# An attention and non-local kernel: v's projection with nested products, softmax denominators taken earlier, another range test

## The chip, the cores and the metric

The kernel runs on one core of a Trainium2 chip. That core has a matrix engine (TensorE, PE in the profile; its weight loads are PEld), a vector engine (VectorE, DVE), a scalar engine (ScalarE, ACT), a general one (GpSimd, POOL), and SyncE (SP), which mostly issues DMA transfers. Sixteen DMA engines do these transfers. The metric is the device time of one launch in microseconds: the median of the runs.

## The reference

Eight images of 512 channels and 32x32 = 1024 pixels pass through two layers, all in fp32. Layer 0 is self-attention with 8 heads of 64 channels and a residual. Layer 1 is a non-local block with a residual, followed by batch norm over all images.

```python
q, k, v = conv1x1(x, Wq, bq), conv1x1(x, Wk, bk), conv1x1(x, Wv, bv)   # 512 -> 512, 8 heads of 64
attn = softmax(einsum('bhdn,bhdm->bhnm', q, k) * 64**-0.5)
x = x + conv1x1(einsum('bhnm,bhdm->bhdn', attn, v), Wp, bp)

g, theta, phi = conv1x1(x, g_w), conv1x1(x, theta_w), conv1x1(x, phi_w)  # 512 -> 256, with biases
f = einsum('bcn,bdn->bcd', theta, phi) / 1024
z = conv1x1(einsum('bcd,bdn->bcn', f, g), W_w, W_b) + x
out = (z - mean(z)) * rsqrt(var(z) + 1e-5) * gamma + beta                # mean, var over images, pixels
```

## The kernel before

**The images in turn.** A loop runs over the images. For image b it does attention (`attention`), then the projections q, v and k of image b+1 in this order (`heads_of`, `values`, `heads_of`), then image b's projection by Wp with the residual (`project`), theta and phi (`theta_phi`), and the rest of the non-local block (`nonlocal_`). The q, k and v of image 0 come before the loop. Batch norm follows at the end (`last_z`).

**Matmuls in fewer products.** A product of two matrices cut 2x2 is done with 7 products of quarters in place of 8 (Strassen's scheme, Winograd's form). `seven` does this; its matmuls stand in line 300. It needs sums of quarters of the weights and of the data. Those of the weights are made once, in image 0 (`weight_sums`), and stored in DRAM beside the quarters as "kept" weights. Each later use loads the whole set again by `load_w` (line 134), in the order of a list `queue`, into one of two buffers. Sums of the data are made on VectorE at each use (`data_sums`, `more_sums`; `inner_parts` for those of a quarter's quarters).

For the weights named in `INNER`, some of the seven products are themselves done by seven smaller ones: three products of WqT and WkT, two of WpT. `nested` does that (line 255). The four large products that stay (`FOUR`) are cut into 16 units, and between these the small steps are interleaved as a table `STEPS` says: none up to unit 2, at most two per unit after that. A dictionary `fills` gives, per unit, VectorE work of other kinds that is to stand there in program order.

PSUM is held as four double banks of 128 x 2 x 512, with tags s0 to s3; a list `free` says which stage takes which one, in what order. A bank is written again only when its last reader is done. q and k are made channel by pixel; v is made pixel by channel ("positions out": the data are the stationary operand, the weights move). In v before, all seven products are of 2 x 4 matmuls with 256 moving columns, 56 in all.

**Attention.** Scores (line 462) and the weighted sums of v (line 488) are matmuls on 64x64 tiles of the array. ScalarE takes the exponential without subtracting a maximum (line 465), and VectorE adds up what the denominators need, eight key blocks into `acc` (lines 469 and 471). For each of eight groups of two heads and half of the pixels, `spread` (lines 499 and 501) folds the 128 partitions of `acc` to 32, by one transfer of SyncE and three accumulating ones of GpSimd, into a buffer `fold`. After every four groups two more transfers fold 128 rows of that to 64.

**Denominators.** `all_denominators` sums the rows of `fold` on TensorE (line 434): two matmuls with 64 columns of a selector `folds8` as weights and 512 moving columns. VectorE takes the reciprocal (line 534, 128x512), SyncE writes one row of each group to DRAM (line 536), and four SyncE transfers of 512 KB read them back into the same buffer, each row spread over 64 partitions (`rows_of`, line 558). Then four multiplications on VectorE (line 571) scale the attention's output `o`. The matmuls, the reciprocal and the transfers are issued after v's product 1 (`norm`), the multiplications after its product 5. The load of k's weights is issued after q, ahead of them, and SyncE issues its transfers one after another in program order. For the last image there is a different path (`denominators`, in two halves), and no further projections.

**The range test.** Since the exponential isn't shifted, the kernel returns whether that was sound; if not, a second kernel (`shifted`) is run. Before, `bound_scores` bounds the scores: the largest |q| and |k| per channel (line 397, eight VectorE reductions an image), a matmul with a matrix `heads` (line 425), a comparison (line 427), and four GpSimd multiplications of q by 0 or 1 (line 429). In the end all flags are reduced.

**Order.** The order of most work is left to a scheduler, which places instructions by program order, readiness and buffers. `pe`, `dve` and `sp` pin an instruction to program order on its engine: all of TensorE's are, and some of VectorE's and SyncE's. The start of image 0 has a fixed VectorE order for the sums that q needs (line 842).

Of the kernel before, what the change touches and what calls it, by code (L numbers as in the profile page):

```python
# [19 lines left out]
BOUND = 60.0  # L20
# [10 lines left out]
def unshifted(ctx: ExitStack, tc: tile.TileContext, a: dict, out: bass.AP):  # L31
# [83 lines left out]
    INNER = {"WqT": (1, 2, 6), "WkT": (1, 2, 6), "WpT": (1, 2)}  # L115
# [8 lines left out]
    def load_w(dma):  # L124

        if not queue:
            return
        name = queue.pop(0)
        half = quarter(name, 0, 0).shape[2]
        t, w = weights_tile(name, half)  # L130
        loaded.append((name, w))
        if name in kept:
            of = kept["plain"] if name == "WpT" and len(queue) == 2 else kept[name]
            ins = dma.dma_start(t[:, :of.shape[1]], of)
            if len(queue) == 1:
                sp(ins)
            return
        corner[name] = block(f"a21_{name}")[:, :, :half]
        for to, m, k in ((w[:, 0], 0, 0), (w[:, 1], 0, 1), (w[:, 2], 1, 1), (corner[name], 1, 0)):
            dma.dma_start(to, quarter(name, m, k))  # L140

    def weights(name, sums_done=False):

        n, w = loaded.pop(0)
        assert n == name
        if name not in kept:
            if not sums_done:
                weight_sums(w, corner[name])
            if name not in ("WqT", "WkT"):
                keep("plain" if name == "WpT" else name, w)  # L150
        return w
# [11 lines left out]
    def keep_inner(name, w):  # L163

        for n in range(len(INNER[name])):
            a11, a12, a22, a21, s2, s3, s4 = inner_blocks(w, name, n)
            for to, l, r, op in ((s3, a11, a21, ALU.subtract), (a21, a21, a22, ALU.add), (s2, a21, a11, ALU.subtract),
                                 (s4, a12, s2, ALU.subtract)):
                nc.vector.tensor_tensor(to, l, r, op)
# [75 lines left out]
    def nested(name, stage, w, data, tags, first, add):  # L245
# [3 lines left out]
        for n, (q, di, begins) in enumerate(goes_to[i] for i in INNER[stage]):  # L249
# [3 lines left out]
            for _, wi, di, s, reads in SEVEN:  # L253
                ps = pair[s % 2 if s < 2 else 1][:, s // 2, n % 2 * 256:(n % 2 + 1) * 256]
                pe(nc.tensor.matmul(ps, a[wi], d[di], start=s not in begun, stop=True, skip_group_check=True))  # L255
                begun.add(s)
                for to, is_first in reads:
                    c = rows(q).start + int(to[0]) - 1
# [4 lines left out]
    def seven(name, w, data, positions_out, first, add, between=None, early=False,  # L263
# [10 lines left out]
        if inner:  # L274
            free[:] = [tags[1], tags[2], tags[3], tags[0]]
            steps = nested(name, inner, w, data, tags[2:], first, add)
# [6 lines left out]
        for n, m in HALVES if three else ((n, None) for n in range(len(products))):  # L283
# [12 lines left out]
            work = [(*part, k) for part in (parts if m is None else parts[m:m + 1]) for k in range(nk)]  # L296
            if by_chunk and what in ("11", "s1t1"):
                work.sort(key=lambda one: one[4])
            for to_ps, at, lhsT, rhs, k in work:
                pe(nc.tensor.matmul(to_ps, lhsT(k), rhs(k), start=(s, at) not in begun, stop=(k == nk - 1),  # L300
                                    skip_group_check=True))
                begun.add((s, at))
                for ahead in (True, False):
# [25 lines left out]
    heads = const.tile([P, P], F32, tag="heads", name="heads")  # L329
    nc.vector.memset(heads, 0.0)  # L330
# [13 lines left out]
    for i in range(WARM):  # L344
        pe(nc.tensor.matmul(ps[:, :P], heads, heads, start=True, stop=True))
# [10 lines left out]
    for i in range(4):  # L356
        nc.vector.memset(folds[i * P // 4:(i + 1) * P // 4, i * D // 4:(i + 1) * D // 4], 1.0)
    folds8 = const.tile([P, D], F32, tag="folds8", name="folds8")
    nc.gpsimd.memset(folds8, 0.0)
    nc.gpsimd.affine_select(out=folds8, in_=folds8, compare_op=ALU.is_gt, fill=1.0, base=1 - P // 8,  # L360
                            pattern=[[-P // 8, 8], [0, D // 8]], channel_multiplier=1)
    nc.gpsimd.affine_select(out=folds8, in_=folds8, compare_op=ALU.is_ge, fill=0.0, base=0,
                            pattern=[[-P // 8, 8], [0, D // 8]], channel_multiplier=1)
    for j in range(2):
        nc.vector.memset(heads[j * D:(j + 1) * D, j * D:(j + 1) * D], 1.0)
    mv = const.tile([P, CC, 2], F32, tag="mv", name="mv")
    gates = const.tile([P, B * NPAIR], F32, tag="gates", name="gates")
# [9 lines left out]
    def heads_of(b, what, w, bias, data, pin=lambda ins: None, later=None, **how):  # L377

        t = mats.tile([P, CC, N], F32, tag=what, name=f"{what}_{b}")
        peak = small.tile([P, CC], F32, tag=f"peak_{what}", name=f"peak_{what}_{b}")  # L380
# [15 lines left out]
        def peak_of(c):  # L396
            ins = nc.vector.tensor_reduce(peak[:, c:c + 1], t[:, c, :], AX.X, ALU.max, apply_absolute_value=True)
            if b == 0 or later is not None:
                dve(ins)

        for c in range(CC):
            if later is None:
                peak_of(c)
            else:
                later.append(lambda c=c: peak_of(c))
        return t, peak

    def values(b, w, data, between=None):
        v = mats.tile([P, NB, C], F32, tag="v", name=f"v_{b}")

        def at(q):
            return v[:, (int(q[1]) - 1) * NB // 2:int(q[1]) * NB // 2, (int(q[0]) - 1) * C // 2:int(q[0]) * C // 2]

        def as_v(ps):
            return ps.rearrange("p h (i f) -> p (h i) f", f=C // 2)

        seven(f"pv_{b}", w, data, True, lambda q, ps: nc.scalar.copy(at(q), as_v(ps)),  # L417
              lambda q, ps: dve(nc.vector.tensor_tensor(at(q), at(q), as_v(ps), ALU.add)), between)
        return v

    def bound_scores(b, q, k, peak_q, peak_k):

        nc.vector.tensor_tensor(peak_q, peak_q, peak_k, ALU.mult)
        ps = next_bank(f"bound_{b}")[:, 0, :]
        pe(nc.tensor.matmul(ps[:, :CC], heads, peak_q, start=True, stop=True))
        gate = gates[:, b * NPAIR:(b + 1) * NPAIR]
        nc.vector.tensor_scalar(gate, ps[:, :CC], BOUND / SCALE, 1.0, ALU.is_le, ALU.mult)  # L427
        for p in range(NPAIR):
            nc.gpsimd.tensor_scalar(q[:, p, :], q[:, p, :], gate[:, p:p + 1], 1.0, ALU.mult, ALU.mult)  # L429
# [6 lines left out]
    def attention(b, q, k, v, near_end, make_f=None):  # L436
# [66 lines left out]
        def spread(u, pin=lambda ins: None, meanwhile=lambda: None):  # L503
# [18 lines left out]
            if i == 3 and not make_f:  # L522
                two = t[:, g, :].rearrange("(r s) n -> s r n", s=2)
                together(t[g * D:(g + 1) * D, 2, :], [two[0], two[1]])

        def all_denominators(ps):
# [4 lines left out]
            t, ps = t[:, 2, :], ps[:, 0, :]  # L531
            columns(ps, folds8, lambda j: t[:, j * 512:(j + 1) * 512])
            ri = t[:, :512]
            nc.vector.reciprocal(ri, ps)
            d = dram2.tile([16, 512], F32, tag="den", name=f"den_d_{b}")
            nc.sync.dma_start(d, ri.rearrange("(a s) n -> a s n", a=16)[:, 0, :])
            d = d.rearrange("(j g i) n -> g j (i n)", j=2, g=2)
            return d[0], d[1]

        def denominators(g, ps):  # L540
# [8 lines left out]
            d = dram2.tile([8, 512], F32, tag=f"den{g}", name=f"den_d_{b}_{g}")  # L549
            nc.sync.dma_start(d, ri.rearrange("(a s) n -> a s n", a=8)[:, 0, :])  # L550
            return d.rearrange("(j i) n -> j (i n)", j=2)
# [8 lines left out]
        def normalize(d):  # L560

            for g in range(2):
                if g not in rows:
                    rows_of(g, d[g])
            r = rows["all"]

            def products():
                for g in range(2):
                    for h in range(NH):
                        at = o["o"][:, 2 * g:2 * g + 2, h * 512:(h + 1) * 512]  # L570
                        dve(nc.vector.tensor_tensor(at, at, r[:, 4 * g + h:4 * g + 4:2, :], ALU.mult))

            return products
# [179 lines left out]
    late, z = {}, {}  # L753
# [90 lines left out]
    q, peak_q = heads_of(0, "q", weights("WqT", True), bq, data, early=True, by_chunk=True)  # L844
    keep_inner("WqT", w_first)
    load_w(nc.sync)
# [5 lines left out]
    w = weights("WkT")  # L852
    k, peak_k = heads_of(0, "k", w, bk, data)
    keep_inner("WkT", w)
    load_w(nc.sync)
    v = values(0, weights("WvT"), data, {3: lambda: bound_scores(0, q, k, peak_q, peak_k)})
    load_w(nc.sync)
    held = {}
    for b in range(B):
# [23 lines left out]
        if not last:  # L883
            later, of_22, of_t4 = [], [], []
# [4 lines left out]
                     8: lambda: (of_22[0](), of_22[1]()), 9: lambda: (of_22[2](), of_22[3]())}  # L889
            q, peak_q = heads_of(b + 1, "q", weights("WqT"), bq, nxt["data"], dve, inner="WqT",  # L890
                                 later=later, fills=fills)
            load_w(nc.sync)

            def norm():
                nxt["products"] = normalize(denominators(next_bank(f"den_{b}")))

            v = values(b + 1, weights("WvT"), nxt["data"], {1: norm, 2: lambda: [one() for one in later], 5: lambda: nxt["products"]()})
# [7 lines left out]
            else:  # L905
                w_p = loaded[1][1]
                for unit, which in ((12, (3, 4)), (14, (5, 6))):
                    fills[unit] = lambda which=which: weight_sums(w_p, corner["WpT"], which, dve)
            later_k = []
            k, peak_k = heads_of(b + 1, "k", weights("WkT"), bk, nxt["data"], later=later_k, inner="WkT",  # L910
                                 fills=fills)
# [3 lines left out]
        else:  # L915
# [4 lines left out]
            normalize(nxt["d"])()  # L920
# [16 lines left out]
        elif b > B - LATE and b != B - 2:  # L937
# [3 lines left out]
                       {5: lambda: b < B - 2 and of_theta.append(f_sums(b, tps[0], 0)), 1: lambda: [one() for one in later_k[:2]], 2: lambda: [one() for one in later_k[2:]],  # L941
                        4: lambda: bound_scores(b + 1, q, k, peak_q, peak_k)})
# [20 lines left out]

    last_z()


    good = const.tile([P, 1], F32, tag="good", name="good")
    nc.vector.tensor_reduce(good, gates, AX.X, ALU.min)
# [215 lines left out]
```

## Time and profile before

| | us |
|---|---|
| median of 3 runs (2145.69 to 2147.35) | 2146.07 |
| span of the profiled execution | 2143.6 |
| busy: TensorE / VectorE / ScalarE / GpSimd | 2119.6 / 1448.4 / 742.8 / 193.2 |
| matmuls of scores (L462), of weighted sums (L488) | 529.4, 528.7 |
| reductions for the peaks, each (L397) | 1.2 |
| GpSimd's multiplications of q, each (L429) | 1.1 |
| from issue to landing: 2368 KB of q's or k's weights | 8.8 |
| from issue to landing: 1792 KB of v's weights | 7.2 |
| from issue to landing: 512 KB of r, each of four | 6.9 |

The profiled execution's span is that of its instructions; the median of the runs lies 2.5 us above it. Busy times are those in which an engine executes; two of them overlap freely. In a group's line, the name left of the arrow is what is written, right of it what is read; then come the shape, the number of instructions, the busy sum and the mean in ns, and the engine's idle time just before them with what ended it. In the chain and in a timeline, a line gives the start in us from the span's beginning and the duration. An image takes about 263 us, so the middle ones can stand for each other.

### The profile page before, as it was taken

The numbers are of one execution on the slowest core, as the hardware profiler recorded it, in microseconds if no ns is written. First come the engines' busy times: TensorE is split into PE (matmuls) and PEld (weight loads), VectorE is DVE, ScalarE is ACT, GpSimd is POOL, SyncE is SP. The second block draws the span as 40 slices with busy tenths as digits, with TensorE's granted clock in tenths as the row PEclk, the third lists the DMA queues.
The fourth block names the chain that finished last, engine by engine and source line by source line (L and its number), as shares of the span: only waits on it lengthen the run. The fifth ranks groups of instructions, "written<-read, shape, count | busy, mean of one in ns | idle before, by whom it ended". The sixth has DMA issues, their size and how long they took to land.

```text
span 2143.6 us, 30444 instructions
## 1 busy us (share of the span) xinstructions
PE 2119.6 (99%) x12654; PEld 1123.3 (52%) x12654; DVE 1448.4 (68%) x1795; ACT 742.8 (35%) x848; POOL 193.2 (9%) x242
## 2 busy tenths in 40 slices
PE   9999999999999999999999999999999999999996
PEld 4534664356733567335673366633666347743462
DVE  6467667667676676766667667676675676756736
ACT  1464104641046310463105621066212652056106
POOL 0111000110001100011001100011000110011000
PEclk9999999999999999999999999999999999999998
DMA  6433443334143331433323342233434235122758
GB/s 242 137 46 58 136 166 127 49 71 129 73 131 49 79 116 73 133 50 83 109 102 109 48 100 99 97 107 50 108 132 161 42 45 139 52 60 39 227 197 341
DMA packets 53969, 231.05 MB, mean 108 GB/s; under 512 B 9792, under 2 KB 16192, under 8 KB 46272
## 3 DMA queue, kind: packets, MB, share of 16 engines
q1 hardware_dynamic: 42144, 199.26, 27.5%
q0 software_dynamic: 10192, 28.46, 11.0%
q8 instruction: 101, 1.65, 0.3%
q10 hardware_dynamic: 1488, 1.32, 0.2%
q14 instruction: 44, 0.36, 0.1%
HBM read 141.84 MB, written 46.27 MB: 88 GB/s over the span
## 4 chain that ended last, share of the span: by engine, by line
PE 96%; ACT 1%; DVE 1%; DMA 1%; issue 0%; SPq 0%; ACTq 0%; DVEq 0%
PE ps L462 21%; PE po L488 21%; PE pv L300 9%; PE ptp L300 9%; PE pp L300 7%; PE pk L300 6%; PE pq L300 5%; PE pg L300 4%; PE pk_in_s L255 3%; PE pq_in_s L255 3%; PE pz L300 2%; PE pf L658 2%; PE pp_in_s L255 2%; PE pwf L713 1%; ACT z L830 1%; PE pf L674 1%
## 5 line engine op out<-in xcount | busy, mean ns | idle before, releaser
L465 ACT ACTIVATE e<-ps 128x1024 f32<-128x1024 f32 x512 | 522.6, 1024 | 431.1 <-PE ps L462 425.6
L471 DVE TENSOR_TENSOR acc<-acc,e 128x1024 f32<-128x1024 f32 x384 | 470.0, 1224 | 143.7 <-ACT e L465 140.3
L462 PE MATMUL ps<-q,k 64*64 64x512 f32 x4096 | 529.4, 589 | 0.0
L488 PE MATMUL po<-e,v 64*64 64x512 f32 x4096 | 528.7, 589 | 0.0
L488 PEld LDWEIGHTS po<-e,v 64*64 64x64 f32 x4096 | 156.6, 133 | 282.9 <-issue 275.4
L462 PEld LDWEIGHTS ps<-q,k 64*64 64x64 f32 x4096 | 155.5, 133 | 283.8 <-issue 274.8
L501 POOL DMA_DIRECT2D fold<-acc x189 | 147.1, 779 | 978.9 <-DMA fold<-acc 576.6
L701 ACT ACTIVATE g<-pg,gb 128x512 f32<-128x512 f32 x31 | 21.3, 687 | 475.4 <-PE pg L300 475.3
L469 DVE TENSOR_TENSOR acc<-e,e 128x1024 f32<-128x1024 f32 x64 | 78.3, 1224 | 136.6 <-ACT e L465 136.6
L300 PE MATMUL pv<-w_WvT,t_x 128*128 128x256 f32 x512 | 116.4, 381 | 0.0
L300 PE MATMUL ptp<-w_tp,t_x 128*128 128x256 f32 x512 | 114.4, 379 | 0.0
L417 ACT COPY v<-pv 128x1024 f32<-128x1024 f32 x32 | 32.4, 1012 | 213.9 <-PE pv L300 213.9
L300 PEld LDWEIGHTS pv<-w_WvT,t_x 128*128 128x128 f32 x512 | 96.6, 190 | 18.5 <-issue 5.7
L300 PEld LDWEIGHTS ptp<-w_tp,t_x 128*128 128x128 f32 x512 | 97.3, 190 | 13.2
L300 PE MATMUL pq<-t_x,w_WqT 128*128 128x512 f32 x200 | 100.1, 592 | 0.8 <-DVE t_x L842 0.8
L300 PE MATMUL pp<-t_o,w_WpT 128*128 128x512 f32 x208 | 100.8, 592 | 0.0
L300 PE MATMUL pk<-t_x,w_WkT 128*128 128x512 f32 x200 | 100.0, 592 | 0.0
L429 POOL TENSOR_SCALAR q<-q,gates 128x1024 f32<-128x1024 f32 x32 | 35.1, 1109 | 718.4 <-DVE gates L427 718.4
L300 PE MATMUL ptp<-w_tp,x 128*128 128x256 f32 x384 | 87.4, 381 | 0.0
L300 PE MATMUL pv<-w_WvT,x 128*128 128x256 f32 x384 | 86.8, 379 | 0.0
L324 DVE TENSOR_TENSOR q<-q,pq_in_s 128x256 f32<-128x256 f32 x119 | 48.6, 420 | 51.1 <-PE pq_in_s L255 38.4
L324 DVE TENSOR_TENSOR k<-k,pk_in_s 128x256 f32<-128x256 f32 x119 | 47.9, 420 | 48.6 <-PE pk_in_s L255 36.0
(195 smaller groups left out, 2348.6 us busy)
## 6 DMA issues: line engine op xcount, KB each, us to landing
fold<-acc POOLq DMA_DIRECT2D x189, 128.0 KB, 3.1
w_WqT<-kept_WqT SPq DMA_DIRECT2D x7, 2368.0 KB, 8.8
w_WkT<-kept_WkT SPq DMA_DIRECT2D x7, 2368.0 KB, 8.8
r<-den_d SPq DMA_DIRECT2D x32, 512.0 KB, 6.9
x<-in_x_dram SPq DMA_DIRECT2D x30, 512.0 KB, 5.7
w_WpT<-kept_WpT SPq DMA_DIRECT2D x6, 2176.0 KB, 8.3
w_WvT<-kept_WvT SPq DMA_DIRECT2D x7, 1792.0 KB, 7.2
w_tp<-kept_tp SPq DMA_DIRECT2D x7, 1792.0 KB, 7.3
```

Of the source, the lines that this page charges most:

```text
L255: pe(nc.tensor.matmul(ps, a[wi], d[di], start=s not in begun, stop=True, skip_group_check=True))
L300: pe(nc.tensor.matmul(to_ps, lhsT(k), rhs(k), start=(s, at) not in begun, stop=(k == nk - 1), skip_group_check=True))
L324: pin(nc.vector.tensor_tensor(at, at, ps if len(ps.shape) == 3 else ps.unsqueeze(1), ALU.add))
L417: seven(f"pv_{b}", w, data, True, lambda q, ps: nc.scalar.copy(at(q), as_v(ps)), lambda q, ps: dve(nc.vector.tensor_tensor(at(q), at(q), a ...
L429: nc.gpsimd.tensor_scalar(q[:, p, :], q[:, p, :], gate[:, p:p + 1], 1.0, ALU.mult, ALU.mult)
L462: pe(nc.tensor.matmul(ps[c * P // 2:(c + 1) * P // 2, j, :], k[r, p, keys], q[r, p, h * 512:(h + 1) * 512], start=True, stop=True, skip_gr ...
L465: nc.scalar.activation(e, ps, AF.Exp, scale=SCALE)
L469: nc.vector.tensor_tensor(accs[u], es[u, 0], e, ALU.add)
L471: ins = nc.vector.tensor_tensor(accs[u], accs[u], e, ALU.add)
L488: pe(nc.tensor.matmul(ps[j * D:(j + 1) * D, r, :], v[keys, m, (2 * p + j) * D:(2 * p + j + 1) * D], e[keys, j, :], start=(m == 0), stop=(m ...
L501: nc.gpsimd.dma_start(to, part_of, accum_op=ALU.add)
L658: pe(nc.tensor.matmul(to, theta[l][:, i, :], phi[r][:, i, :], start=(i == 0), stop=(i == NB // 2 - 1), skip_group_check=True))
```

## The change

- **v.** WvT joins `INNER`: for images 1 to 7, four large products remain (64 records of matmuls, 256 moving columns), and three are done by 7 small steps each, of two matmuls with 128 moving columns. The kept set for v's weights grows from 1792 to 2368 KB. Image 0 makes the additional sums (`keep_inner`). v's results are read from PSUM by three ScalarE copies and three VectorE additions of 128x1024, plus four copies and 17 additions of 128x256.
- **Denominators.** They come at unit 14 of q, in a bank of q's own. A selector `folds4` sums four rows at once from the 128 rows that `spread` leaves, so the second fold's transfers go: eight matmuls with 32 columns of weights and 256 moving columns, on four column tiles. The reciprocal is 128x256 and pinned on VectorE. ScalarE's queue writes it to DRAM; SyncE reads the rows with two transfers of 1 MB instead of four of 512 KB. These are pinned on SyncE ahead of the load of k's weights.
- **Multiplications of o.** They stand at v's units 10, 11, 12 and 14.
- **Range test.** Peaks, bound, flags and the multiplications of q go. Each image's reciprocals stay in DRAM, and in the end they are loaded (nine small transfers) and compared with 1e-20 and 1e20 on VectorE.
- **Image 0.** More of VectorE's work is pinned, and q's inner sums with the load of v's weights come after the sums of k's weights. The warming matmuls read a tile `zeros`.

```diff
-    INNER = {"WqT": (1, 2, 6), "WkT": (1, 2, 6), "WpT": (1, 2)}
+    INNER = {"WqT": (1, 2, 6), "WkT": (1, 2, 6), "WvT": (1, 2, 6), "WpT": (1, 2)}
 ...
             ins = dma.dma_start(t[:, :of.shape[1]], of)
+            pin(ins)
 ...
                 ps = pair[s % 2 if s < 2 else 1][:, s // 2, n % 2 * 256:(n % 2 + 1) * 256]
-                pe(nc.tensor.matmul(ps, a[wi], d[di], start=s not in begun, stop=True, skip_group_check=True))
+                if positions_out:
+                    ps = ps.rearrange("p (i f) -> p i f", f=P)
+                    for i in range(2):
+                        pe(nc.tensor.matmul(ps[:, i, :], d[di][:, i * P:(i + 1) * P], a[wi], start=s not in begun and not i,
+                                            stop=True, skip_group_check=True))
+                else:
+                    pe(nc.tensor.matmul(ps, a[wi], d[di], start=s not in begun, stop=True, skip_group_check=True))
 ...
-    def bound_scores(b, q, k, peak_q, peak_k):
-
-        nc.vector.tensor_tensor(peak_q, peak_q, peak_k, ALU.mult)
-        ps = next_bank(f"bound_{b}")[:, 0, :]
-        pe(nc.tensor.matmul(ps[:, :CC], heads, peak_q, start=True, stop=True))
-        gate = gates[:, b * NPAIR:(b + 1) * NPAIR]
-        nc.vector.tensor_scalar(gate, ps[:, :CC], BOUND / SCALE, 1.0, ALU.is_le, ALU.mult)
-        for p in range(NPAIR):
-            nc.gpsimd.tensor_scalar(q[:, p, :], q[:, p, :], gate[:, p:p + 1], 1.0, ALU.mult, ALU.mult)
 ...
             together(to[:, g, :], parts)
-            if i == 3 and not make_f:
-                two = t[:, g, :].rearrange("(r s) n -> s r n", s=2)
-                together(t[g * D:(g + 1) * D, 2, :], [two[0], two[1]])
 ...
-            t, ps = t[:, 2, :], ps[:, 0, :]
-            columns(ps, folds8, lambda j: t[:, j * 512:(j + 1) * 512])
-            ri = t[:, :512]
-            nc.vector.reciprocal(ri, ps)
-            d = dram2.tile([16, 512], F32, tag="den", name=f"den_d_{b}")
-            nc.sync.dma_start(d, ri.rearrange("(a s) n -> a s n", a=16)[:, 0, :])
-            d = d.rearrange("(j g i) n -> g j (i n)", j=2, g=2)
-            return d[0], d[1]
+            ps, of = ps[:, 0, :256], P // 4
+            for g in range(2):
+                for i in range(4):
+                    pe(nc.tensor.matmul(ps[i * of:(i + 1) * of, :], folds4[:, g * of:(g + 1) * of],
+                                        t[:, g, i * 256:(i + 1) * 256], start=(g == 0), stop=(g == 1),
+                                        skip_group_check=True))
+            ri = t[:, 2, :256]
+            dve(nc.vector.reciprocal(ri, ps))
+            d = dram.tile([of, 256], F32, tag=f"den{b}", name=f"den_d_{b}")
+            nc.scalar.dma_start(d, ri.rearrange("(x s) n -> x s n", s=4)[:, 0, :])
+            own.append((dens[:, b * 64:(b + 1) * 64], d.rearrange("x (y n) -> (x y) n", y=4)))
+            return d.rearrange("(j x) m -> j (x m)", j=2)
 ...
+                r = foldp.tile([P, 4096], F32, tag="fold", name=f"r_{b}")
+                for j in range(2):
+                    sp(nc.sync.dma_start(r[j * D:(j + 1) * D, :], d[j].partition_broadcast(D)))
 ...
-    q, peak_q = heads_of(0, "q", weights("WqT", True), bq, data, early=True, by_chunk=True)
-    keep_inner("WqT", w_first)
-    load_w(nc.sync)
+    q = heads_of(0, "q", weights("WqT", True), bq, data, dve, early=True, by_chunk=True)
 ...
-    w = weights("WkT")
-    k, peak_k = heads_of(0, "k", w, bk, data)
+    w = weights("WkT", pin=dve)
+    keep_inner("WqT", w_first)
+    load_w(nc.sync)
+    k = heads_of(0, "k", w, bk, data, dve)
 ...
-                     8: lambda: (of_22[0](), of_22[1]()), 9: lambda: (of_22[2](), of_22[3]())}
+                     8: lambda: (of_22[0](), of_22[1]()), 9: lambda: (of_22[2](), of_22[3]()),
+                     14: lambda: nxt.update(products=normalize(denominators(bank(free[0], f"den_{b}"))))}
 ...
-            v = values(b + 1, weights("WvT"), nxt["data"], {1: norm, 2: lambda: [one() for one in later], 5: lambda: nxt["products"]()})
+            v = values(b + 1, weights("WvT"), nxt["data"], inner="WvT",
+                       fills={unit: lambda i=i: nxt["products"][i]() for i, unit in enumerate((10, 11, 12, 14))})
 ...
+    good, sane = const.tile([P, 1], F32, tag="good", name="good"), block("sane")[:, 0, :]
+    nc.vector.tensor_scalar(sane, dens, 1.0 / SANE, 1.0, ALU.is_ge, ALU.mult)
+    nc.vector.scalar_tensor_tensor(sane, dens, SANE, sane, ALU.is_le, ALU.mult)
+    nc.vector.tensor_reduce(good, sane, AX.X, ALU.min)
```

## The prediction

> **What bounds the kernel now.** I read the page's busy shares first, then the shares of the chain that ended last.
>
> ```profile
> PE 2119.6 (99%) x12654; PEld 1123.3 (52%) x12654; DVE 1448.4 (68%) x1795; ACT 742.8 (35%) x848; POOL 193.2 (9%) x242
> PE 96%; ACT 1%; DVE 1%; DMA 1%; issue 0%; SPq 0%; ACTq 0%; DVEq 0%
> ```
>
> TensorE works for 2119.6 of 2143.6 us, and the chain is its work for 96%. The remaining 24 us are start and tail. Next the list of waits, TensorE's own:
>
> ```profile
> PE warm_ps L345 <- DVE heads L330: 1.1, 1, 1.1
> PE pq L300 <- DVE t_x L842: 0.8, 1, 0.8
> PE den L434 <- PE pg L300: 0.5, 1, 0.5
> PE den L434 <- DVE bp L193: 0.2, 1, 0.2
> ```
>
> These 2.6 us are all that it waits for. Time can be won only by giving TensorE less to do, and it is lost wherever a new wait is longer than its cover. So I took the chain in order of time around v of one middle image (start, duration, instructions), with a piece of another product with the same small shape:
>
> ```profile
> 738.27 0.86 PE pq L300 x2
> 739.56 6.91 PE pv L300 x32
> 746.46 1.01 PE den L434 x4
> 747.47 17.46 PE pv L300 x80
> 764.94 3.43 PE pk L300 x8
> ...
> 843.92 6.25 PE pf L658 x56
> ```
>
> v runs from 739.56 to 764.94: 25.38 us, the denominators' 1.01 among them. Every fp32 matmul leaves two records; one over 256 columns takes 6.91/32 = 0.2159 us, and one of L658, whose 128x128 weights meet 128 columns, 6.25/56 = 0.1116 us.
>
> The groups with shapes told apart give what else is removed:
>
> ```profile
> L534 DVE RECIPROCAL fold<-den 128x512 f32<-128x512 f32 x7 | 23.5, 3358 | 32.6 <-PE den L434 32.6
> L425 PE MATMUL bound<-peak_q,heads 128*128 128x4 f32 x16 | 2.2, 211 | 0.0
> ```
>
> Last, SyncE's timeline over q and v of that image:
>
> ```profile
> 739.59 0.33 SPq L134 DMA_DIRECT2D w_WkT<-kept_WkT  x1
> 750.91 0.50 SPq L536 DMA_DIRECT2D den_d<-fold  x1
> 752.75 2.56 SPq L558 DMA_DIRECT2D r<-den_d  x4
> 764.97 0.33 SPq L134 DMA_DIRECT2D w_WpT<-kept_WpT  x1
> ```
>
> and windows of one microsecond within the two large transfers (the last two columns are the DMA engines' share and GB/s):
>
> ```profile
> 743.00:744.00 1.00, 1.00 (x7) 0.87 (x6) 0.00 (x0) 0.95 (x1) 0.00 (x0) 1.00 0.97 417
> 757.00:758.00 1.00, 1.00 (x6) 0.89 (x5) 0.00 (x0) 0.00 (x0) 0.00 (x0) 1.00 1.06 221
> ```
>
> k's weights leave before the denominators are known and move at 417 GB/s. The rows r move at 221 GB/s with all engines busy, so their 2.1 MB take about 9.1 us. In the new order the weights stand behind them.
>
> **What the Trainium skill says.** Its page "TensorE: Matmul & The Clock Gate", section "LDWEIGHTS (loading the stationary operand)", gives a load as columns/1.2 ns, whatever the contraction: 107 ns for 128 columns, 27 ns for 32. The pace of 111.6 ns over 128 columns agrees: load and stream are about equal there, so halving the columns still halves the time. "TensorEngine Tiling (Array Packing)", section "Key Properties", says that tiles work independently of each other and that a change of tiling mode drains the array. The trace agrees on both: 64x64 tiles over 512 columns run at 107.3 ns a record, a quarter of 429.5, and around the four den records some 0.2 us goes on switching. "DMA: Bandwidth & Descriptors", section "Rules for kernel authors", says that transfers into two halves of the partitions share the same 16 engines. Hence I expect two transfers of 1 MB to stream no faster than four of 512 KB; no run here shows it yet.
>
> **The change part by part.**
>
> *v by smaller products* (images 1 to 7). 112 records become 64 of 256 columns and 84 of 128 columns: 64 x 0.2159 + 84 x 0.1116 = 13.82 + 9.37 = 23.19 us. With the denominators gone from v, 25.38 - 23.19 = 2.19 us is saved there. The bound from above for the small ones is the recorded duration of one weight load, 192 ns, should loads not hide: then 84 x 0.192 = 16.1 us and v costs 4.5 us more. L658 has the same shapes and doesn't show it, so I take 0.1116.
>
> *Denominators in q.* 4 records of 512 columns on 64-column tiles become 16 of 256 columns on 32-column tiles. If four tiles run side by side, 4 rounds x 0.2159 = 0.86, with some 0.34 for switching 1.2 us. If only two do, 16 x 0.108 + 0.34 = 2.05 us; if none, 3.7. 64x64 tiles do run by four, but these share all their rows; I take 1.4. So v and denominators give 2.19 - 1.4 = 0.79 us an image, times 7: **-5.5 us**.
>
> *Range test.* Eight matmuls of L425 leave, with the gap they cut: 0.21 us each, **-1.7 us**. The eight peaks an image of 1.2 us on VectorE and four POOL multiplications of 1.1 us go too; nothing on TensorE waited for them, so they are worth nothing but room. The new test at the end (three VectorE operations over 128x512, nine small loads) fits into 2.64 us in which VectorE stood idle between the last statistics and the normalisation; its matmul has TensorE to itself. Without that cover it would cost up to 2 us.
>
> *Start.* VectorE's line L169 waited 1.86 us for k's weights ahead of the sums that the 0.8 us wait of L842 ends on; those sums now come first: **-0.8 us**. The later place of q's weights' sums and of the load of v's weights in image 0 has slack.
>
> *Fold.* Two SyncE/POOL transfers per group of heads go; they were hidden. The last fold lands at about 731.2 (here; in the tightest image 3.9 us before need), and the denominators now read at 738.1 instead of 746.5: 3.9 to 6.9 us remain. Their bank was read last by VectorE, until 737.56: 0.5 us remain.
>
> *VectorE in v.* New are 17 additions of 128x256 (0.34 to 0.42 us) for the small products and the four multiplications o<-o,r (1.22 us) inside v, at units 10, 11, 12 and 14 of 16. Gone are the peaks, 1.7 us of the reciprocal and one copy. The last blocks are read about 0.1 us before TensorE wants their banks. I put small stalls at 0.1 us an image: **+0.7 us** (range -0 to +4).
>
> *Rows and weights, the new wait.* den done at 739.4 to 739.9, reciprocal (half of 3358 ns, 1.7 us) at 741.1 to 741.7, written by ScalarE's queue and landed 1.84 us later as between L536 and L558 now; first transfer of r issued at 743.1 to 743.7. Before, r was complete 12.5 us after its first issue (489.85 to 502.35 in the image where VectorE waited for it): 755.6 to 756.2. The first multiplication can run at about 756.4 to 757.0 and TensorE needs the bank read behind it some 0.4 us later, so the slack is about 1.2 us. Behind r on SyncE stands only the load of k's weights: issued at 744.4, streaming from 753.5 to 759.5 at some 400 GB/s, landed at 761.5 to 762, while k starts at 764: 2.3 us of slack. Behind the reciprocal on VectorE stand the last additions to q, behind the write on ScalarE the copies of v; both have several us. If r is late by more than its slack, VectorE's queue stops, v's blocks aren't read, and TensorE stalls about 1:1 in seven images.
>
> **Sum:** -5.5 - 1.7 - 0.8 + 0.7 = -7.3 us. The profiled execution's span is 2143.6, so 2136.3 after; the median of the runs, 2146.07, lies 2.5 us over the span, so **2138.8 us**.
>
> **Rivals.**
>
> *r is late.* The slack of 1.2 us rests on a sum of six terms, and 2.1 MB share the engines with other loads. Against it: two issues instead of four save 1.2 us of issuing. Late by 1 us more than the slack costs 7 us: 2145.8; by 0.5, 2142.3.
>
> *The denominators' tiles run by two:* + 0.65 x 7 = 4.6 us: 2143.4.
>
> *Slower: k's weights land late.* They wait on SyncE until r is issued and then share 16 engines with it. Should they move at r's rate of 221 GB/s (10.9 us) from r's end at 755.9, they land near 767 plus 2, some 4.6 us after k wants them: seven times, 32 us, about 2171. It decides from a landing 3.9 us later than worked out (2.3 us of slack, 7.3/7 to use up the gain, 4.3/7 to reach 0.2%). Against it: a copy of 2.4 MB by itself has moved at 417 GB/s.
>
> *Slower too: weight loads don't hide* in the small v products: 2138.8 + 7 x 6.7 = 2186.
>
> *The change does what it says, with no stall and den at 1.2:* 2138.8 - 0.7 - 1.4 = 2136.7, which is the low side of the forecast.
>
> **How the numbers follow.** About 0.2% (4.3 us) is what a measurement of this kernel tells from no change: faster is below 2141.8, slower above 2150.4. Forecast with its low side 0.50 (own range 2135.5 to 2141.5); r late 0.22 (2140 to 2149); tiles by two 0.11 (2141 to 2145); k's weights late 0.13 (2146 to 2175); loads that don't hide 0.04. Faster: 0.50, 0.10 of r late and 0.05 of the tiles, 0.65. Slower: 0.10, 0.04 and 0.01 of r late, 0.15. Same: 0.20. Range 2135 to 2150; outside stay most of the late weights, the loads, and about 0.04 below.
>
> **What would show it.** Right: v spans about 23.2 us and is followed by pk without a gap; den's 16 records end within 1.4 us of their start; the waits list has no TensorE wait on VectorE's `v` or on `w_WkT`; no L425; the wait on L842 is gone. Wrong: pv or pv_in waiting for VectorE, with VectorE's idle time before the multiplications put down to r<-den_d; pk waiting for w_WkT<-kept_WkT; records of the small products at 0.13 us or more; den taking 2 us; or a new wait where the start was reordered.

## The result and the profile after

The changed kernel takes 2139.35 us (median of 7 runs, 2138.81 to 2139.72) against 2146.07: a ratio of 0.9969 with an interval of 0.9958 to 0.9979, 6.7 us less. In a second series on another occasion it took 2139.0 us against 2145.49, ratio 0.9971 (0.9960 to 0.9981). The forecast was 2138.8 us. The profiled execution's span went from 2143.6 to 2137.9 us. I read the new profile in the order of the old one. First the page's busy shares and the chain's shares by engine:

```profile
PE 2114.1 (99%) x12974; PEld 1124.5 (53%) x12974; DVE 1411.6 (66%) x1855; ACT 746.5 (35%) x869; POOL 144.9 (7%) x193
PE 95%; DVE 3%; ACT 1%; issue 1%; DMA 0%; DVEq 0%; SPq 0%; ACTq 0%
```

TensorE is busy 5.5 us less, though it issues 320 instructions more. VectorE has grown from 1% to 3% of the chain: that is new. It is not a loss of that size, for the chain also runs over VectorE while TensorE is still at work; what was lost has to be read from the stages. TensorE's list of waits:

```profile
PE warm_ps L358 <- DVE zeros L343: 1.1, 1, 1.1
PE den L427 <- PE pg L311: 0.6, 1, 0.6
PE pk_in_s L262 <- DVE k L337: 0.3, 1, 0.3
PE den L524 <- DVE bp L194: 0.2, 1, 0.2
PE pp L311 <- DVE o L574: 0.2, 1, 0.2
```

The wait of the start (L842 before) is gone, and no wait on a transfer took its place. Two small ones are new, 0.3 us in k and 0.2 us in the last image's projection by Wp. The list does not show what the chain of the middle image shows at the end of v:

```profile
736.85 1.00 PE den L524 x16
737.85 1.06 PE pq L311 x2
739.34 3.45 PE pv L311 x16
742.79 0.45 PE pv_in_s L259 x4
...
755.95 0.46 PE pv_in_s L259 x4
757.37 1.14 DVE o L574
...
759.36 0.06 DVE o L574
759.42 0.99 issue
760.41 1.22 DVE v L421
...
761.73 0.43 DVE v L421
762.16 0.04 issue
762.21 0.71 PE pv_in_s L259 x4
762.92 3.44 PE pk L311 x8
```

The denominators take 1.00 us for 16 records, 62 ns each, and the two q records behind them 1.06 instead of 0.86 (the change of shape). The four records of a small step take 0.45 us, some 112 ns each, as L658's did. But the last step starts late: the chain leaves TensorE, runs over multiplications of o and additions to v on VectorE, and comes back at 762.21. (The 0.99 us of "issue" lie within the multiplication that runs on VectorE from 759.28 to 760.50.)

From the starts of each stage's first matmul in TensorE's timeline, for that middle image:

| stage, us | before | after |
|---|---|---|
| q, with den in it after | 22.91 | 24.10 |
| v, with den in it before | 25.38 | 23.58 |
| k | 22.80 | 22.87 |
| theta and phi, with the bound before | 24.40 | 24.17 |

(The timeline puts v's and k's first matmuls 0.17 us ahead of where the chain has them; the differences are the same.) Summed over the run: q, den and v -4.2 us, k +0.7, the bound's matmuls -1.8 (v of image 0 among them), q of image 0 +0.1. That is -5.2 us, and the last matmul of all starts 5.16 us earlier. The other 0.5 us of the span lie behind it, in the tail of transfers.

The transfers went as worked out. SyncE's timeline, and below it the list of issues from 741 to 765 us (KB each, us from issue to landing):

```profile
741.55 1.12 SPq L565 DMA_DIRECT2D r<-den_d  x2
742.77 0.53 SPq L134 DMA_DIRECT2D w_WkT<-kept_WkT  x1
```

```profile
w_WkT<-kept_WkT SPq DMA_DIRECT2D x1, 2368.0 KB, 17.9
r<-den_d SPq DMA_DIRECT2D x2, 1024.0 KB, 9.5
```

k's weights land at 760.7 and k starts at 762.75: 2.1 us of slack, where I had put 2.3. The two transfers of r in this image land 7.3 and 11.7 us after their issue (the list has the median), the second at 753.7; the first multiplication starts at 755.01, 1.3 us later. But not every image has that much. In the image ahead of it the two transfers and the first multiplication stand so:

```profile
L565 SPq DMA_DIRECT2D r<-den_d x2: 476/532/588, 479.3 to 479.9; - x2
DMA to landing us min/median/max: 7.3/10.1/13.0
492.90 1.23 DVE L574 TENSOR_TENSOR o<-o,r 128x1024 f32<-128x1024 f32 x1
```

The second lands at 492.88, 13.5 us after the first issue, and VectorE uses it 0.02 us later. In the last image whose v is made in the loop (v from 1775.6 on) it is 0.14 us. v takes 23.58 us there too, so nothing was lost, but there was nothing to spare.

### The profile page after: what moved, and what is told of

It reads as the page before. It is cut to its first block, busy times and chain, and to the rows that moved or that the text cites. A ratio compares the mean times of both kernels' runs of the same rounds, so it can differ in the third digit from the quotient of the medians.

```text
span 2137.9 us, 31084 instructions
## 1 busy us (share of the span) xinstructions
PE 2114.1 (99%) x12974; PEld 1124.5 (53%) x12974; DVE 1411.6 (66%) x1855; ACT 746.5 (35%) x869; POOL 144.9 (7%) x193
## 4 chain that ended last, share of the span: by engine, by line
PE 95%; DVE 3%; ACT 1%; issue 1%; DMA 0%; DVEq 0%; SPq 0%; ACTq 0%
PE ps L455 21%; PE po L481 21%; PE ptp L311 9%; PE pp L311 7%; PE pq L311 6%; PE pk L311 5%; PE pv L311 5%; PE pg L311 4%; PE pq_in_s L262 3%; PE pk_in_s L262 3%; PE pz L311 2%; PE pv_in_s L259 2%; PE pf L661 2%; PE pp_in_s L262 2%; PE pwf L716 1%; DVE v L421 1%
## 5 line engine op out<-in xcount | busy, mean ns | idle before, releaser
L494 POOL DMA_DIRECT2D fold<-acc x189 | 144.7, 766 | 1838.8 <-DMA fold<-acc 760.7
L311 PE MATMUL pv<-w_WvT,t_x 128*128 128x256 f32 x400 | 100.7, 380 | 0.0
L421 DVE TENSOR_TENSOR v<-v,pv_in_s 128x256 f32<-128x256 f32 x119 | 49.1, 420 | 64.5 <-PE pv_in_s L259 50.3
L311 PEld LDWEIGHTS ptp<-w_tp,x 128*128 128x128 f32 x384 | 73.0, 190 | 13.3 <-issue 3.8
L311 PEld LDWEIGHTS pv<-w_WvT,t_x 128*128 128x128 f32 x400 | 69.6, 191 | 6.0
L311 PE MATMUL pp<-o,w_WpT 128*128 128x512 f32 x144 | 67.8, 593 | 0.2 <-DVE o L574 0.2
```

The source lines that it names most:

```text
L494: nc.gpsimd.dma_start(to, part_of, accum_op=ALU.add)
```

## Experiments

Each but `later_free_k` starts from the changed kernel. They were measured in three series. In the first (`again`, `v_seven`, `test_back`, `mult_later`) times stand beside the changed kernel's, 2139.0 us; in the second (`mult_early`, `k_first`, `four_r`, `start_old`) beside a variant that behaves like it, `four_r` with 2139.52 us. The third (`later_free_k`, `mult_in_k`, `no_mult`) has neither; the kernel before took 2145.48 us in it and 2145.49 in the first, so the first's times are used.

**The changed kernel again.**

> The changed kernel once more, to stand beside the others. Its first profile shows the stages from q to the end of v at 47.68 us in a middle image (48.29 before) and a start whose first matmuls of q ran at half pace (four records of 0.86 us instead of 0.43 between 4.6 and 7.1 us). My theory: those 1.05 us are the execution's, not the change's, and vary from one execution to the next; then this profile's q of image 0 takes 24.1 to 25.2 us by chance. Rival: the reordered start causes it; then q takes 25.2 us here again. Time about 0.9969 of before.

2139.0 us. The stages from q to v repeat to 0.02 us. q of image 0 takes 24.64 us here, 24.17 to 25.20 in the eleven profiles with the new start. Here no matmul of q runs at half pace (0.43 us apart from 4.4 us on, with two waits for q's weights), so the half pace of the first profile was not the change's.

**v by seven products.**

> Only the nested products of v are undone: seven products of 256 columns again, the multiplications of o after product 5 as before; denominators, rows, range test and start stay new. My theory (records times pace): v takes 24.2 to 24.4 us instead of 23.58, nothing waits, k takes 22.80 instead of 22.86: +0.55 to 0.75 us in each of seven images, +4 to +5 us against the changed kernel. Rival: the gain is that of work taken from VectorE and GpSimd, and v's smaller products give it back in stalls: within 1 us of the changed kernel, or faster.

```diff
-    INNER = {"WqT": (1, 2, 6), "WkT": (1, 2, 6), "WvT": (1, 2, 6), "WpT": (1, 2)}
+    INNER = {"WqT": (1, 2, 6), "WkT": (1, 2, 6), "WpT": (1, 2)}
 ...
-    keep_inner("WvT", w)
 ...
-            v = values(b + 1, weights("WvT"), nxt["data"], inner="WvT",
-                       fills={unit: lambda i=i: nxt["products"][i]() for i, unit in enumerate((10, 11, 12, 14))})
+            v = values(b + 1, weights("WvT"), nxt["data"], between={5: lambda: [one() for one in nxt["products"]]})
```

2144.34 us, +5.3; ratio to before 0.9993 (0.9984 to 1.0001). From the first matmul of v to that of k, in the middle image:

```profile
739.90 3.62 PE L311 MATMUL pv<-w_WvT,x 128*128 128x256 f32 x16
764.08 3.60 PE L311 MATMUL pk<-x,w_WkT 128*128 128x512 f32 x8
```

v takes 24.18 us, the pace of its 112 records, instead of 23.58: 4.15 us in seven images. The rest of the 5.3 us lies, in the two profiles, mostly in the start and in the last image's projection by Wp, which took 24.03 us in `again`, 24.53 here and 24.49 in the changed kernel's first profile. k stays at 22.86, against what I expected. So most of the whole gain hangs on the nested products, and k's 0.06 us aren't theirs. With seven products, q, den and v together take 48.3 us, as before the change: moving the denominators by itself won nothing on TensorE.

**The old range test.**

> Only the range test of before is put back in place of the new one (peaks of q at units 5 to 8 of v, peaks of k and the bound in theta and phi, four GpSimd multiplications). My theory: eight matmuls at 0.23 us each, +1.8 us against the changed kernel; the peaks fall into time in which VectorE stood idle. Rival: VectorE's room decides; with 4.6 us more of it in v, v's blocks are read late and TensorE stalls by 0.5 us or more in each image, +5 us and more.

The edit puts `peaks`, `bound_scores` and the final reduction of flags back, without the new test. 2141.19 us, +2.2; theta and phi with the bound take 24.40 us again in image 1, +1.8 us by stages over the run. v stays at 23.59 although VectorE does this in it:

```profile
747.02 1.21 DVE L413 TENSOR_REDUCE peak_q<-q 128x1 f32<-128x1024 f32 x1
748.81 1.21 DVE L413 TENSOR_REDUCE peak_q<-q 128x1 f32<-128x1024 f32 x1
750.27 2.34 DVE L413 TENSOR_REDUCE peak_q<-q 128x1 f32<-128x1024 f32 x2
```

4.8 us of VectorE's work in v and 4.4 us of GpSimd's in each image cost nothing; the bound's eight matmuls cost 1.8. The rival, VectorE's room as such, falls. Room counts by its place, as the next run shows.

**Two multiplications later.**

> The third multiplication of o moves from v's unit 12 to 14 and the fourth from v's unit 14 to k's unit 0; nothing else. My theory: v's 23.58 us are 23.19 by records and the rest is the wait for VectorE's reading of a block at v's end (0.12 us shown as idle, some more as a lengthened last step), so v becomes 23.2 to 23.4 us and k stays at 22.86 or a little more: -1 to -2.5 us. Rival: the rest is the change between shapes within v, which stays: no change; or the late multiplication makes k wait, and the time rises by up to 2 us.

```diff
-                       fills={unit: lambda i=i: nxt["products"][i]() for i, unit in enumerate((10, 11, 12, 14))})
+                       fills={unit: lambda i=i: nxt["products"][i]() for i, unit in enumerate((10, 11, 14))})
 ...
+            fills[0] = lambda: nxt["products"][3]()        # k's fills
```

2136.42 us, -2.6. The middle image's first matmuls of v and k:

```profile
737.91 3.62 PE L311 MATMUL pv<-w_WvT,x 128*128 128x256 f32 x16
761.10 3.60 PE L311 MATMUL pk<-x,w_WkT 128*128 128x512 f32 x8
```

v takes 23.19 us in all seven images, which is the sum of its records; k stays. VectorE's timeline of the changed kernel at the end of v shows the cause:

```profile
758.42 0.94 DVE L421 TENSOR_TENSOR v<-v,pv_in_s 128x256 f32<-128x256 f32 x2
759.28 1.22 DVE L574 TENSOR_TENSOR o<-o,r 128x1024 f32<-128x1024 f32 x1
760.41 1.21 DVE L421 TENSOR_TENSOR v<-v,pv 128x1024 f32<-128x1024 f32 x1
761.73 0.75 DVE L421 TENSOR_TENSOR v<-v,pv_in_s 128x256 f32<-128x256 f32 x2
```

From 758.42 VectorE has no break longer than 0.1 us. The multiplication at unit 12 (759.28) stands ahead of the large addition and of two small ones; the first of these ends near 762.2, and TensorE's last step, which the chain shows released by it, starts at 762.21. Moved two units on, the multiplication delays no read that TensorE waits for. The fourth multiplication, which the edit moves too, starts at 762.40 in the changed kernel, behind that step's start, so it isn't what held it.

**k's additions unpinned as well.**

> As mult_later, and VectorE's additions to k are no longer pinned to program order in images 1 to 7, so that one addition of 128x1024 comes ahead of a sum instead of behind it. My theory: the wait of 0.3 us in image 0's k and the 0.06 us in the others go (k 22.80 instead of 22.86, 23.08 instead of 23.40): -0.7 us against mult_later, some 2135.8 us. Rival: these came from something else, or the order then delays another block: no change or slower.

```diff
-            k = heads_of(b + 1, "k", weights("WkT"), bk, nxt["data"], dve, inner="WkT", fills=fills)
+            k = heads_of(b + 1, "k", weights("WkT"), bk, nxt["data"], inner="WkT", fills=fills)
```

This edit stands on top of `mult_later`. 2135.53 us; ratio to before 0.9952 (0.9939 to 0.9966). k is back at 22.80 us, 23.08 in image 0's turn, and its wait has left TensorE's list:

```profile
PE warm_ps L358 <- DVE zeros L343: 1.1, 1, 1.1
PE den L427 <- PE pg L311: 0.6, 1, 0.6
PE den L524 <- DVE bp L194: 0.2, 1, 0.2
PE pq L311 <- DMA w_WqT<-in_WqT_dram: 0.2, 1, 0.2
```

The stages show -0.7 us for k. The times alone would not: 0.9 us lie within both intervals. This version beats both kernels, by 10 us and by some 3.5.

**The multiplications earlier.**

> The four multiplications of o stand at v's units 7, 8, 9 and 10 instead of 10, 11, 12 and 14. My theory: r lands about 12 us after its first issue, near 754 in the middle image, and VectorE comes to unit 7 near 750.6; VectorE then stands for some 3.4 us in front of r, v's blocks are not read, and TensorE stalls nearly 1:1 once the banks are full: 2 to 3.5 us an image, +14 to +25 us against the changed kernel. Rival: the banks give several us of slack, and the time rises by less than 5 us.

```diff
-                       fills={unit: lambda i=i: nxt["products"][i]() for i, unit in enumerate((10, 11, 12, 14))})
+                       fills={unit: lambda i=i: nxt["products"][i]() for i, unit in enumerate((7, 8, 9, 10))})
```

2169.39 us, +30. VectorE's timeline, with its wait in brackets:

```profile
759.32 0.42 DVE L421 TENSOR_TENSOR v<-v,pv_in_s 128x256 f32<-128x256 f32 x1 [0.89 <-PE pv_in_s L259]
763.84 2.36 DVE L574 TENSOR_TENSOR o<-o,r 128x1024 f32<-128x1024 f32 x2 [4.11 <-DMA r<-den_d]
```

SyncE issued r at 751.47 in this execution, and VectorE went on 12.4 us later. v took 27.5 to 29.8 us, 3.9 to 6.2 more than 23.58. In five images VectorE waited 4.0 to 4.3 us for r and v lost 3.9 to 4.2; in the two where r comes latest it waited 5.2 and 5.4 us and v lost 6.1 and 6.2. So the stall is about 1:1, as expected, and up to 0.9 us more where the wait is longest; that the multiplications, close together behind the wait, add this is likely, but no run shows it. What I had too small was the wait itself, 3.4 us.

**k's weights ahead of r.**

> The load of k's weights is issued ahead of r on SyncE, as before the change; everything else stays new. My theory: r's packets queue behind 2.4 MB of weights, r lands 2.5 to 4 us later, the first multiplication waits for it and TensorE stalls for 2 to 3 us in each image: +14 to +21 us. Rival: r moves at its own slow rate and both transfers overlap, so that r lands within the 1 us of slack: no change.

```diff
-                     14: lambda: nxt.update(products=normalize(denominators(bank(free[0], f"den_{b}"))))}
+                     14: lambda: nxt.update(d=denominators(bank(free[0], f"den_{b}")))}
 ...
             load_w(nc.sync, sp)
+            nxt["products"] = normalize(nxt["d"])
```

2176.18 us, +37; v takes 28.4 to 30.1 us. The direction was right, the mechanism was not. SyncE's timeline:

```profile
750.89 0.33 SPq L134 DMA_DIRECT2D w_WkT<-kept_WkT  x1
758.72 1.12 SPq L565 DMA_DIRECT2D r<-den_d  x2
```

r isn't queued behind the weights: it isn't even issued until 7.8 us later, when they have passed. What it waits for is the write of the denominators, 32 KB on ScalarE's own queue, issued at 751.23. The landing times of that write (L530; least, median, most), first in the changed kernel, then in this one:

```profile
DMA to landing us min/median/max: 1.7/1.7/1.7
```

```profile
DMA to landing us min/median/max: 7.2/7.3/8.3
```

r itself then takes the 12.5 us from first issue to last landing that it took before (758.72 to 771.27). So the order on SyncE keeps 2.4 MB of weights from getting in front of a small write on another queue. The Trainium skill ("DMA: Bandwidth & Descriptors", section "Rules for kernel authors") says that transfers issued from SP, ACT and GpSimd run on the same 16 engines and interleave. That they share the engines is what this run shows; the interleaving did not let 32 KB pass in less than 7.2 us.

**Four transfers of r, written by SyncE.**

> SyncE writes the denominators instead of ScalarE, and r comes by four transfers of 512 KB instead of two of 1 MB. My theory: two more issues of 0.55 us make the last landing about 1 us later, which uses up the slack: 0 to +3 us against the changed kernel. Rival: the larger transfers move faster by themselves; then r lands 2 us later or more and the time rises by 7 us and more.

```diff
-            nc.scalar.dma_start(d, ri.rearrange("(x s) n -> x s n", s=4)[:, 0, :])
+            sp(nc.sync.dma_start(d, ri.rearrange("(x s) n -> x s n", s=4)[:, 0, :]))
 ...
-                    sp(nc.sync.dma_start(r[j * D:(j + 1) * D, :], d[j].partition_broadcast(D)))
+                    for h in range(2):
+                        at = slice(h * 2048, (h + 1) * 2048)
+                        sp(nc.sync.dma_start(r[j * D:(j + 1) * D, at], d[j, at].partition_broadcast(D)))
```

2139.52 us, ratio 0.9971 (0.9959 to 0.9982), the changed kernel's own. All stages of the middle images are equal to 0.02 us and the multiplications run at their places. The queue that writes and the size of the transfers, changed together, made no difference: with `k_first`, it is their place ahead of the weights that counts.

**The old order of image 0.**

> Only image 0's order is that of before: VectorE's additions for q's inner sums, q and k aren't pinned, and q's inner sums with the load of v's weights come right after q. My theory: the wait of 0.8 us for the data's sums comes back, and q of image 0 takes 25.1 us where it took 24.6 to 25.2: 0 to +0.8 us against the changed kernel. Rival: the reordering is worth nothing because the first matmuls wait for q's weights anyway: no difference in q's 24.6 to 25.2 us.

The edit undoes the diff's part on image 0. 2141.43 us, ratio 0.9979 (0.9972 to 0.9987). q of image 0 takes 26.0 us, and the wait is back:

```profile
PE pq L311 <- DVE t_x L845: 1.3, 1, 1.3
```

With the old order q of image 0 took 26.0 us here and 25.14 in the kernel before; with the new one 24.17 to 25.20 in eleven profiles, 24.66 in the mean. So the reordering is worth some 0.9 us, though single executions overlap; by times it is 1.9, with intervals that overlap too. That the wait returns with the old order is shown, so the rival, that the order is worth nothing, does not stand; its size stays rough.

**All multiplications in k.**

> All four multiplications of o stand in k, at its units 0, 1, 2 and 3, none in v. My theory: v is at its records' 23.19 us; VectorE is held for 4.9 us at k's start and k's first small steps may wait for their banks: v gains 0.39 us, k loses 0 to 0.8 us: -2.7 to +3 us against the changed kernel. Rival: something other than the multiplications holds the end of v, and it stays at 23.58 us.

The fills of v are dropped, and `nxt["products"]` stands at units 0 to 3 of k's fills. 2149.03 us, slower than before the change: ratio 1.0017 (1.0010 to 1.0023). v is at 23.19, but k takes 24.67 us, 1.8 more:

```profile
PE pk_in_s L262 <- DVE k L337: 9.2, 15, 0.8
```

I had allowed k 0.8 us in all; it lost more than twice that. VectorE runs three multiplications in a row just as k's first small steps fill their banks.

**No multiplications.**

> The multiplications of o by the reciprocals are left out for images 0 to 6 (that part of the softmax is not computed); r is still transferred. It measures what the multiplications cost TensorE. My theory: v takes 23.19 us as in mult_later, k 22.8 to 22.9: -2.5 to -3.2 us against the changed kernel. Rival: with the wait for r gone too, more is won than the 0.39 us an image, which would show that r's landing still cost time: -5 us or more.

2136.15 us; v takes 23.19, k 22.86. That is `mult_later` to 0.3 us. So the multiplications cost the changed kernel 0.39 us an image by the place of the third one, and r's landing costs nothing.

## Why the prediction was right

**The time.** 2138.8 forecast, 2139.35 measured, inside the likeliest case's own range. Its terms did not all hold: the denominators cost less than forecast and the waits more, and that the two nearly offset each other was luck. One sign that I had named did not come: v is not 23.2 us long, and its last step waits for VectorE.

| term, us | forecast | measured by stages |
|---|---|---|
| v and denominators, without waits | -5.5 | -6.9 |
| waits in v and k | +0.7 | +3.4 |
| range test | -1.7 | -1.8 |
| start | -0.8 | +0.1 in the first profile, -1.0 to -0.2 in the others |
| sum | -7.3 | -5.2 with the first profile's start |

The stages are those of one execution each, and the first profile's start was its slowest; the medians differ by 6.7 us.

*v by smaller products*: 23.19 us by records, and 23.19 measured as soon as nothing waits. The price from L658, a line of another product with the same shape, held to the last digit.

*Denominators in q*: I took 1.4 us between 1.2 and 3.7; it is 1.20 (24.10 - 22.91). Four column tiles do run side by side: 62 ns a record against 215.9 over the whole array. This agrees with the Trainium skill's "TensorEngine Tiling (Array Packing)", section "Key Properties", on tiles working independently. So the term is 2.19 - 1.20 = 0.99 us an image, -6.9. The rival "tiles by two" is out. (Its price comes to 2.07 us and that of no overlap to 3.8, where I wrote 2.05 and 3.7; nothing hangs on it.)

*VectorE in v*: this is the step that was mis-sized. I saw that the last blocks are read "about 0.1 us before TensorE wants their banks", and still put 0.1 us an image. It was 0.39, 2.7 us in all. What I did not work out is where each multiplication falls among the reads: the one at unit 12 adds 1.2 us just where three reads follow each other. The change also pins VectorE's additions to k in images 1 to 7, which the list of the change leaves out and of which I had said nothing; it cost another 0.7 us. The stated range of this term, up to +4, holds both.

*Rows and weights*: r's issue was worked out at 743.1 to 743.7 and came at 741.55. But this image's q starts at 715.07 instead of 716.48, since time had been won by then; counted from there, the issue comes after 26.5 us, with 26.6 to 27.2 worked out. In the middle image r lands 1.3 us ahead of its first use; my figures gave 0.8 (the 1.2 us count 0.4 more, until TensorE needs the bank). k's weights have 2.1 us against 2.3. What I had wrong is that one image stood for all. I took the 12.5 us to r's landing from a single image of the old trace, though another showed 13.4 us there already, with VectorE waiting for r:

```profile
1541.76 2.40 SPq L558 DMA_DIRECT2D r<-den_d  x4
1555.16 2.36 DVE L571 TENSOR_TENSOR o<-o,r 128x1024 f32<-128x1024 f32 x2 [1.21 <-DMA r<-den_d]
```

In the tightest image of the changed kernel r takes 13.5 us and has 0.02 us left. That "r is late" did not happen is in part luck. What it costs is shown by `mult_early`, 30 us for a wait of 4 to 5.4 us an image. "k's weights late" did not happen either; no run made them late. As for the order on SyncE, in `k_first` I expected r's own packets to suffer; it shows that the small write does.

*Range test and start*: `test_back` and `start_old` show both by undoing them. The range test is as priced; the start's size stays rough.

*Fold and the test at the end* were costed at nothing, and no stage shows any cost of theirs; no run undid them by themselves. The test's three operations run from 2082.5 to 2084.4, in the idle time that I had named, of which 0.87 us is left; it lies among the statistics, not behind the last of them. The loads of the reciprocals do not wait for the end: the scheduler puts one behind k's weights in each image (743.35 in the middle one).

## What to carry to other kernels

Where one engine is busy for 99% of the span, a change is worth its records times their pace, taken from a line of the same shape; what remains to be found is the place where a helper engine now reads a bank too late. Look for that in the helper's timeline at the end of the stage, operation by operation: VectorE's busy share fell, 4.8 us more work in one place cost nothing, and one multiplication two units too early cost 0.39 us in each image. And put a small transfer on which a chain hangs ahead of the large ones, on whatever queue they are. A slack that was worked out for one image has to be looked up in the tightest: here the middle image had 1.3 us to spare and the one before it none.

## What the hardware showed unexpectedly

A write of 32 KB on ScalarE's queue landed after 1.7 us by itself and after 7.2 to 8.3 us when 2.4 MB of weights had been issued on SyncE's queue 0.3 us before.

The first matmuls of q ran at half pace for a time that differs between executions of kernels with the same start. In the changed kernel's profile weight loads take 0.34 us and stand 0.85 us apart until 7.1 us, as here, and 0.19 and 0.43 us after that:

```profile
5.50 0.34 PEld L311 LDWEIGHTS pq<-x,w_WqT 128*128 128x128 f32 x1 [0.52 <-issue]
```

The granted clock in windows of two microseconds reads 1.00 there and doesn't show it. Three records of q take 2.46 us (4.64 to 7.10) where they take 1.29 later on: 1.2 us, more than the start's reordering is worth, and it hid that gain in the first comparison. Where nothing runs at half pace, as in `again`, waits for q's weights take part of that time instead, so q of image 0 differs by 1 us between executions. What sets the half pace no run shows.
